# Four transformer layers in one kernel: `by` loads issued by GpSimd, another order at the ends of the feed-forwards, key norms tile by tile

## The chip, the cores and the metric

The kernel runs on one core of a Trainium2 chip. A time is the device time of one launch in microseconds, the median of three runs. Beside the timed runs there is one profiled execution, from which every row, gap and duration below is taken; the page gives its own time and its span.

The core has a matrix engine (TensorE, PE in the profile, whose weight loads are listed as PEld), a vector engine (VectorE, DVE), a scalar engine (ScalarE, ACT), a general one (GpSimd, POOL) and a queue engine (SyncE, SP) that here only issues transfers. A DMA can be issued by SyncE or by GpSimd; the profile lists the first kind's queue as hardware_dynamic and the second's as software_dynamic.

## The reference

The input x has 1024 tokens of 256 numbers. Eight stages follow one another, each `x = layernorm(x + stage(x))`: four times an attention and then a feed-forward, each pair of another design. Everything is float32.

- attn0: 16 heads, 4 key heads, window of 64, rotary positions, two softmaxes subtracted. ffn0: 8 experts, 2 per token.
- attn1: 16 heads of 128, causal, biases. ffn1: weights rounded to three values, hidden width 1024, a root mean square norm over the hidden row.
- attn2: 16 heads of 16, causal. ffn2: hidden width 2048, weights stored as 4-bit codes with a scale per 32 of them (dequantized as table value times scale), gelu gate.
- attn3: 16 query heads, 4 key heads of 128; queries and keys are divided by their root mean square over the head's 128 numbers before the scores. ffn3: 64 experts of width 64, 8 per token, and one shared expert with its own gate:

```
comb[token, expert] = top-8 probability, renormalized      # 0 for the other experts
out = sum over experts of (silu(x Wg) * (x Wu)) Wd * comb[:, expert]  +  gate * shared expert
```

ffn3 computes every expert for every token and multiplies by `comb`, which is zero where the expert was not chosen. These multipliers are called `factors` in the kernel.

## The kernel before, in words

x lies in SBUF as 8 tiles of 128 tokens, and its transpose xT, which the projections read, as 256 rows by 1024 tokens. Much is done by halves of 512 tokens (tiles 0 to 3, tiles 4 to 7). `transpose_two(t)` (L178) transposes two tiles of x on TensorE and copies them into xT (L185). `project` (L159) multiplies a weight by 512 columns of xT; `project_rows` (L166) gives rows of 128 tokens instead.

The order of work. In the attention stages it is written out by hand: `in_order` fixes the order of every engine's instructions as the program issues them. A `Pipe` there holds a list of units (the scores of one head for one tile of queries: matmul L274, maximum L254 on VectorE, exponent L259 on ScalarE, normalization L267 on GpSimd, transposition by L371 and a DMA, or by TensorE in L390 for some, and the product with values L408) and fills the matmul time that remains with other pieces of work, projections above all, by their estimated costs. In the feed-forward stages a scheduler decides the order within the program's own dependencies and priorities.

**Feed-forwards 2 and 3** share `Kit.ffn` (L289 to L323). The hidden width is cut into chunks of 128 (16 in ffn2, 33 in ffn3, the last one the shared expert). `add_up(i, half)` projects one chunk's gate and up for 512 tokens (4 matmuls of L159, which the trace shows as 8 entries), calls `hidden` for the activation, and multiplies by the down weights into two accumulators in PSUM (2 matmuls of L307, 4 entries). The loop does chunk i of the first half and chunk i - lag of the second half (lag 3 in ffn2, 4 in ffn3), so that the second half trails. At the last chunk the first half is complete: `add_ffn(acc, 0)` copies the accumulators out of PSUM (L332), transposes them on TensorE (L336), adds them to x (L240) and norms x's first half (L209, L210, L227, L228, L213). ffn1 has its own loop of the same form (L1395 to L1402) with 8 chunks and `finish(half)`, which first sums the squares of the hidden rows by matmuls and takes a root on ScalarE.

**hidden of ffn3** (L2196 to L2206): ScalarE computes silu of the gate (L2203), VectorE multiplies by up (L2204) and then by `by` (L2205). `by` is a tile of 128 rows by 512 tokens, in which the factors of the chunk's two experts stand 64 times each. It is loaded from `factors` in DRAM by a DMA whose source repeats a row 64 times (L2201): 66 loads of 256 KB, into 8 rotating buffers, issued by SyncE, which also issues the weight loads (L97). The factors are written to DRAM at the end of attn3 by the steps of the router.

**attn1** carries a second task, `beside`: the generator `ffn2_weights` dequantizes ffn2's weights long before they are used. It has 157 steps, over 24 half tiles of 128 x 512: VectorE operations L1836, L1840, L1844 and L1849, a GpSimd multiply by scales L1854, and DMAs issued by GpSimd for codes and scales (L1805, L1808, L1818, L1821) and for the result (L1859). After each of the 128 units of attn1 the loop takes one step, and two after every fourth unit.

**attn3** starts by transposing x. Its list of pieces then has, for the first half: key rows of four tiles (`make_rows`: L166, copied by L2002, squared and summed by ScalarE in L2005), values of four tiles (L166, L2033), `norm_rows` of the half, queries (L159), keys (transposed normed rows); and the same for the second half, which runs between the first units of the softmax. `norm_rows` raises the mean squares to the power -1/2 (`power`: L220 on VectorE, L221 on GpSimd, 128 x 16 for a half) and multiplies the rows by them on GpSimd (L2013, 128 x 2048 for a half). GpSimd also does two of the softmax's steps in this stage, a small product (L256) and the normalization (L267).

The stages' list in `four_layers` (L2232) says which pairs of tiles are transposed ahead of each stage: all four in attn3, none in ffn2 and ffn3.

Of the kernel before, what the change touches and what calls it, by code (L numbers as in the profile page):

```python
# [31 lines left out]
P = 128  # L32
# [10 lines left out]
class Kit:  # L43
# [245 lines left out]
    def ffn(self, chunks, count, hidden, before=iter(()), lag=LAG):  # L289

        nc = self.nc
        acc = [self.wide() for _ in range(NC)]
        held = {}

        def add_up(i, half):
            size, gate, up, down, more = held[i] if half == 0 else held.pop(i)
            g, u = self.bank()[:size], self.bank()[:size]  # L300
            self.project(g, gate, half * HALF, HALF)
            next(before, None)
            self.project(u, up, half * HALF, HALF)
            next(before, None)
            h = hidden(g, u, half, more)
            for m in range(NC):
                nc.tensor.matmul(  # L307
                    acc[m][:, half * HALF : (half + 1) * HALF],
                    lhsT=down[:, m * P : (m + 1) * P], rhs=h, start=i == 0, stop=i == count - 1,
                )  # L310

        for i in range(count + lag):
            if i < count:
                held[i] = next(chunks)
                add_up(i, 0)
            if i == lag - 1:
                for _ in before:
                    pass
            if i == count - 1:
                self.add_ffn(acc, 0)  # L320
            if i >= lag:
                add_up(i - lag, 1)
        self.add_ffn(acc, 1)  # L323

    def add_ffn(self, acc, half, scale=None):
# [740 lines left out]
def attn1(k, a):  # L1066
# [171 lines left out]
    with k.in_order(transfers=True):  # L1238
        for t in range(NT):
            two = k.tile("ot", [P, 2, D])  # L1240
            for i in range(2):
                gathered.append(two[:, i, :])
                k.gather(gathered[-1], results, slots[:, i * NT + t : i * NT + t + 1])

        for t, count in ((0, 0), (2, 3), (4, 4), (6, 5)):
            add_results(t)
            for i in range(count - 1):
                project_next()
            take_root(t)
            if count:  # L1250
                project_next()
            close(t)
        for count, (g, h, half, s) in enumerate(units):
            now[:] = g, h
            if count == 96:
                pipe.base = 1.2
            if (h, half) == (1, 0) and g < 3:
                if s == 0:
                    loading = load(g + 1)
                next(loading, None)  # L1260
            if s == 0:
                ensure(make_queries, g, 15)
                ensure(make_keys, g, h, half)
            blocks = 4 * half + s + 1
            if s % 2 == 0:
                pipe.reach(count // 2 - 3)
                pair = Pair(k, (blocks, blocks + 1), on_pe=(g, h) == (3, 3))
            pipe.unit(
                queries[g][:, h, (blocks - 1) * P : blocks * P],
                lambda lo, n: keys[g, h][:, lo : lo + n], blocks, pair, s % 2,  # L1270
                masked=g == 3,
            )
            if s % 2:
                pipe.then(attend(g, h, half, s // 2, pair))
            pipe.fill()
            for _ in range(2 if count % 4 == 3 else 1):
                next(beside, None)
        for _ in pipe.drain():
            pass
        for _ in beside:  # L1280
            k.catch_up()
        k.catch_up()
# [55 lines left out]
def ffn1(k, a):  # L1338
# [56 lines left out]
    for i in range(8 + k.LAG):  # L1395
        if i < 8:
            add_up(i, 0)
        if i == 7:
            finish(0)
        if i >= k.LAG:  # L1400
            add_up(i - k.LAG, 1)
    finish(1)  # L1402


# [494 lines left out]
def attn3(k, a):  # L1899
# [107 lines left out]
                accum_out=total[half][:, t % 4 * 4 + h : t % 4 * 4 + h + 1],  # L2007
            )

    def norm_rows(half):  # L2010
        norm = k.power(total[half], 16, 1e-6, 1.0 / 128)
        heads = raw[half].rearrange("p t (h d) -> p (t h) d", h=4)
        nc.gpsimd.tensor_tensor(  # L2013
            heads, heads, norm.unsqueeze(2).to_broadcast([P, 16, P]), ALU.mult
        )

    def make_keys(half, h):
# [48 lines left out]
        factors[g, half] = k.power(ps[:, ::32], 16, 128e-6, tag="factor")  # L2066


    pieces = [(make_rows, t) for t in range(4)]
    pieces += [(make_values, t) for t in range(4)]  # L2070
    pieces += [(norm_rows, 0)]
    pieces += [(make_queries, 0, 0, h) for h in range(4)]
    pieces += [(make_sums, 0, 0)]
    pieces += [(make_keys, 0, h) for h in range(4)]
    pieces += [(make_factors, 0, 0)]
    pieces += [(make_rows, t) for t in range(4, 8)] + [(norm_rows, 1)]
    pieces += [(make_values, t) for t in range(4, 8)]
    pieces += [(make_queries, 0, 1, h) for h in range(4)]
    pieces += [(make_sums, 0, 1)]
    pieces += [(make_keys, 1, h) for h in range(4)]  # L2080
# [89 lines left out]
def ffn3(k, a):  # L2170


    nc = k.nc

    def chunks():
        gu = wd = None
        for p in range(32):
            if p % 2 == 0:
                gu = k.weights(
                    [P, NC, 512],  # L2180
                    a["L3_ffn_gate_up"][:, p * 256 : (p + 2) * 256].rearrange(
                        "(c p) f -> p c f", p=P
                    ),
                )
            if p % 4 == 0:
                wd = k.weights([P, 4, D], a["L3_ffn_down"][:, p * D : (p + 4) * D])
            at = (p % 2) * 256
            yield (
                P, lambda c, w=gu, s=slice(at, at + P): w[:, c, s],
                lambda c, w=gu, s=slice(at + P, at + 2 * P): w[:, c, s], wd[:, p % 4, :], p,  # L2190
            )
        gu = k.weights([P, NC, P], a["L3_ffn_shared_gate_up"].rearrange("(c p) f -> p c f", p=P))
        wd = k.weights([64, D], a["L3_ffn_shared_down"])
        yield (64, lambda c: gu[:, c, :64], lambda c: gu[:, c, 64:], wd, 32)

    def hidden(g, u, half, p):  # L2196
        n = g.shape[0]

        by = k.tile("by", [P, HALF])[:n]
        rows = k.factors[2 * p : 2 * p + n // 64, half * HALF : (half + 1) * HALF]  # L2200
        nc.sync.dma_start(out=by, in_=rows.unsqueeze(1).to_broadcast([n // 64, 64, HALF]))  # L2201
        s, h = (k.tile("t2", [P, HALF])[:n] for _ in range(2))
        nc.scalar.activation(s, g, AF.Silu)  # L2203
        nc.vector.tensor_tensor(h, s, u, ALU.mult)  # L2204
        nc.vector.tensor_tensor(h, by, h, ALU.mult)  # L2205
        return h  # L2206

    k.ffn(chunks(), 33, hidden, (step for steps in k.closing for step in steps), lag=4)


# [14 lines left out]
def four_layers(ctx: ExitStack, tc: tile.TileContext, a, out):  # L2225
# [3 lines left out]
    for stage in STAGES:  # L2229
        with k.scope(**SCOPES[stage]):  # L2230

            mine = {ffn0: (), attn1: (), ffn1: (), ffn2: (), attn2: (0, 2), ffn3: ()}  # L2232
            for t in mine.get(stage, range(0, NT, 2)):
                k.transpose_two(t)
            stage(k, a)
            if stage == attn1:
                k.layernorm()
# [75 lines left out]
```

## Time and profile before

| | us |
|---|---|
| median of three runs | 2238.06 (2237.61 to 2240.51) |
| the profiled execution's own time | 2230.16 |
| its span | 2228.5 |
| TensorE busy in it | 2037.2 |
| granted TensorE clock, mean | 0.972 |

By stage, from the trace (bounds by the stages' first and last matmuls, rounded):

| stage | from, to | length | PE busy | DVE busy | ACT busy | POOL busy | DMA share |
|---|---|---|---|---|---|---|---|
| attn0 | 0, 296 | 296 | 241.8 | 230.5 | 153.0 | 106.8 | 0.38 |
| ffn0 | 296, 395 | 99 | 79.3 | 56.8 | 37.7 | 29.5 | 0.39 |
| attn1 | 395, 906 | 511 | 488.3 | 346.3 | 213.3 | 175.3 | 0.44 |
| ffn1 | 906, 967 | 61 | 54.9 | 32.8 | 36.3 | 20.1 | 0.16 |
| attn2 | 967, 1196 | 229 | 199.8 | 136.8 | 101.3 | 32.8 | 0.15 |
| ffn2 | 1196, 1379 | 183 | 176.9 | 87.3 | 45.7 | 0.0 | 0.06 |
| attn3 | 1379, 1838 | 459 | 426.6 | 295.5 | 211.8 | 157.1 | 0.35 |
| ffn3 | 1838, 2228.5 | 390.5 | 369.6 | 113.4 | 50.4 | 0.7 | 0.20 |

How to read it: busy times are microseconds within the stage; the DMA share is the mean busy share of the core's 16 DMA engines. In timeline rows the first number is the start from the span's beginning, the second the time that the row's instructions took together, then engine, line, operation, the tile written and the tiles read, the shape and how many instructions; in brackets stands how long the engine had been idle before, and what released it. SPq and POOLq rows are issues of DMAs. A row of waits gives the total, how many times, and the longest. In the 40 slices a digit is the busy share in tenths. The times of the table add to the span; the 1.7 us between the span and the execution's own time lie outside of what the trace shows.

### The profile page before, as it was taken

How to read it: one execution, taken by the hardware profiler on the slowest of the kernel's cores; microseconds unless marked ns; L12 is line 12 of the kernel's file. 1: busy time of each engine (PE TensorE's matmuls, PEld its weight loads, DVE VectorE, ACT ScalarE, POOL GpSimd, SP SyncE). 2: the span in 40 equal slices, each digit the busy share in tenths (PEclk: the TensorE clock that was granted, in tenths of full speed). 3: DMA queues.
4: the chain of work that ended last, by engine and by line, in shares of the span. 5: the costliest groups of instructions: out<-in, count | busy, mean ns of one | idle time of the engine just before them, and what ended most of it. 6: DMA issues, size and time to landing. Idle time of an engine off the chain costs nothing.

```text
span 2228.5 us, 24592 instructions
## 1 busy us (share of the span) xinstructions
PE 2037.2 (91%) x7893; PEld 1191.4 (53%) x7893; DVE 1299.4 (58%) x2588; ACT 849.6 (38%) x2230; POOL 522.3 (23%) x771
## 2 busy tenths in 40 slices
PE   7988768899999997988988998899999989999997
PEld 3655544576766665754434443466666665433343
DVE  6898756677777664456754444277777664222223
ACT  3656424453444433444462223654444441111111
POOL 5343131333333332402110000433333320000000
PEclk9999879999999999999999999999999999999998
DMA  6222443253545542105000000034355321222211
GB/s 183 76 72 58 136 130 109 64 148 102 145 108 161 144 103 78 38 29 181 1 2 10 29 30 0 24 95 111 93 141 125 91 53 63 76 76 84 76 65 44
DMA packets 152520, 186.88 MB, mean 84 GB/s; under 512 B 31460, under 2 KB 115240, under 8 KB 152392
## 3 DMA queue, kind: packets, MB, share of 16 engines
q1 hardware_dynamic: 142808, 160.25, 26.2%
q0 software_dynamic: 9584, 25.05, 3.7%
q8 instruction: 64, 1.05, 0.2%
q14 instruction: 64, 0.52, 0.1%
HBM read 85.24 MB, written 17.44 MB: 46 GB/s over the span
## 4 chain that ended last, share of the span: by engine, by line
PE 62%; DVE 9%; DMA 7%; ACT 3%; issue 3%; POOL 2%; SPq 1%; DVEq 0%; POOLq 0%; ACTq 0%
PE bank L159 19%; PE wide L274 9%; PE bank L408 8%; PE wide L307 6%; DMA by<-factors 5%; PE bank L166 4%; PE bank L1179 2%; DVE turned L371 2%; PE bank L1616 2%; PE bank L856 2%; PE bank L1019 1%; DMA pt<-turned 1%; PE bank L1354 1%; POOL p L267 1%; PE wide L1629 1%
## 5 line engine op out<-in xcount | busy, mean ns | idle before, releaser
L159 PE MATMUL bank<-xT,w 128*128 128x512 f32 (+2 forms) x1488 | 629.2, 563 | 4.1 <-DVE xT L185 3.0
L159 PEld LDWEIGHTS bank<-xT,w 128*128 128x128 f32 (+1 forms) x1488 | 283.1, 194 | 275.1 <-issue 254.3
L371 DVE STREAM_TRANSPOSE turned<-p 128x128 f32<-128x128 f32 (+7 forms) x232 | 283.5, 1222 | 76.0 <-DMA pt<-turned 40.3
L274 PE MATMUL wide<-k,q 128*128 128x512 f32 (+3 forms) x768 | 293.7, 492 | 18.3 <-ACT p L259 17.5
L267 POOL TENSOR_SCALAR p<-p,st 128x128 f32<-128x128 f32 (+7 forms) x256 | 190.5, 744 | 475.3 <-DVE st L266 474.8
L408 PE MATMUL bank<-pt,v 128*128 128x256 f32 x1216 | 279.4, 371 | 8.0 <-DMA pt<-turned 5.7
L408 PEld LDWEIGHTS bank<-pt,v 128*128 128x128 f32 x1216 | 225.9, 191 | 60.6 <-issue 21.0
L254 DVE TENSOR_REDUCE st<-wide 128x1 f32<-128x128 f32 (+7 forms) x256 | 193.4, 756 | 47.1 <-PE wide L279 40.1
L307 PE MATMUL wide<-t,w 128*128 128x512 f32 (+1 forms) x392 | 196.7, 626 | 17.0 <-DVE t L2205 11.8
L274 PEld LDWEIGHTS wide<-k,q 128*128 128x128 f32 x768 | 139.5, 191 | 135.3 <-issue 92.9
L259 ACT ACTIVATE p<-wide,st,factor 128x128 f32<-128x128 f32 (+7 forms) x128 | 106.4, 831 | 213.5 <-POOL st L256 210.6
L2204 DVE TENSOR_TENSOR t<-t,bank 128x512 f32<-128x512 f32 (+1 forms) x66 | 45.3, 686 | 238.8 <-PE bank L159 238.8
L259 ACT ACTIVATE p<-wide,st 128x128 f32<-128x128 f32 (+7 forms) x128 | 94.9, 741 | 230.1 <-DVE st L254 211.9
L2203 ACT ACTIVATE t<-bank 128x512 f32<-128x512 f32 (+1 forms) x66 | 39.4, 597 | 305.5 <-PE bank L159 279.5
L307 PEld LDWEIGHTS wide<-t,w 128*128 128x128 f32 (+1 forms) x392 | 67.8, 191 | 134.3 <-DVE t L2205 58.4
L779 ACT ACTIVATE e<-wide,st 128x128 f32<-128x128 f32 x256 | 90.0, 377 | 74.3 <-DVE st L787 65.6
L166 PE MATMUL bank<-w,xT 128*128 128x512 f32 (+2 forms) x288 | 118.0, 547 | 0.0
L249 DVE TENSOR_TENSOR wide<-wide,causal 128x128 f32<-128x128 f32 x192 | 55.9, 291 | 98.7 <-PE wide L274 97.5
L1641 ACT ACTIVATE pt<-wide 128x1024 f32<-128x1024 f32 (+3 forms) x96 | 75.6, 811 | 69.9 <-PE wide L1635 68.1
L166 PEld LDWEIGHTS bank<-w,xT 128*128 128x128 f32 x288 | 52.6, 196 | 44.0 <-issue 40.3
L1593 DVE TENSOR_REDUCE st<-wide 128x2 f32<-128x1024 f32 x64 | 64.3, 1020 | 20.0 <-PE wide L1589 10.2
L845 PE MATMUL bank<-w,ot 128*128 128x256 f32 x256 | 67.4, 411 | 6.8 <-ACT ot L839 5.5
(307 smaller groups left out, 2788.4 us busy)
## 6 DMA issues: line engine op xcount, KB each, us to landing
by<-factors SPq DMA_DIRECT2D x64, 256.0 KB
pt<-turned SPq DMA_DIRECT2D x60, 240.0 KB
pt<-turned SPq DMA_DIRECT2D x60, 176.0 KB
pt<-turned SPq DMA_DIRECT2D x156, 64.0 KB
w<-in_L_ffn_gate_up_dram SPq DMA_DIRECT2D x16, 512.0 KB
pt<-turned SPq DMA_DIRECT2D x28, 256.0 KB
pt<-turned SPq DMA_DIRECT2D x60, 112.0 KB
pt<-turned SPq DMA_DIRECT2D x28, 224.0 KB
```

The lines of the kernel that those rows point to most:

```text
L159: self.nc.tensor.matmul(out, lhsT=weight(c), rhs=self.xcols(c, lo, n), start=c == 0, stop=c == NC - 1)
L166: self.nc.tensor.matmul(out, lhsT=self.xcols(c, lo, n), rhs=weight(c), start=c == 0, stop=c == NC - 1)
L254: nc.vector.tensor_reduce(top, scores[:, :n], axis=AX.X, op=ALU.max, negate=True)
L259: nc.scalar.activation(probs[:, :n], scores[:, :n], AF.Exp, bias=top, scale=1.0 if scale is None else scale, accum_out=total,)
L267: self.nc.gpsimd.tensor_scalar(probs[:, :n], probs[:, :n], total, 1.0, ALU.mult, ALU.mult)
L274: self.nc.tensor.matmul(s[:, lo : lo + m], lhsT=query, rhs=key(lo, m), start=True, stop=not masked or lo + m < n, skip_group_check=masked,)
L307: nc.tensor.matmul(acc[m][:, half * HALF : (half + 1) * HALF], lhsT=down[:, m * P : (m + 1) * P], rhs=h, start=i == 0, stop=i == count - 1,)
L371: k.nc.vector.transpose(squares.rearrange("p b (k q) -> p b k q", q=32), probs[:, :n].rearrange("p (k i b) -> p b k i", b=4, i=32),)
L408: self.k.nc.tensor.matmul(out.rearrange("p (a q) -> p a q", q=32) if first else out.rearrange("p (s a q) -> p s a q", s=2, q=32), lhsT=val ...
L779: nc.scalar.activation(e[:, r, f, b, :], sc[:, r, f, b, :], AF.Exp, bias=top[:, at : at + 1], accum_out=total[:, at : at + 1],)
L845: nc.tensor.matmul(y, lhsT=oT[:, i % 2 * 2 + i // 2].rearrange("p b n -> p (b n)"), rhs=wo[:, i, :], start=i == 0, stop=i == 3,)
L1641: nc.scalar.activation(two[:, :, lo:], sc[:, :, lo:], AF.Exp)
```

## The change

Four edits, independent of each other.

1. In `Kit.ffn`, and likewise in ffn1's loop, the second half's piece `add_up(i - lag, 1)` comes ahead of `add_ffn(acc, 0)` (or `finish(0)`) in the last first-half round, instead of after it.
2. In attn1 the loop takes two steps of `beside` after three of every five units and one after the other two (1.6 a unit), instead of two after one of every four (1.25 a unit).
3. In attn3 `norm_rows` works on one tile (128 x 4 and 128 x 512) and comes after the next tile's rows; the second half's values come tile by tile between rows and norm. x's tiles 4 to 7 are transposed after the first half's last norm piece, instead of ahead of the stage.
4. In ffn3 the `by` loads are issued by GpSimd instead of SyncE.

```diff
@@ Kit.ffn
             if i == lag - 1:
                 for _ in before:
                     pass
+            if i >= lag:
+                add_up(i - lag, 1)
             if i == count - 1:
                 self.add_ffn(acc, 0)
-            if i >= lag:
-                add_up(i - lag, 1)
         self.add_ffn(acc, 1)
@@ attn1
             pipe.fill()
-            for _ in range(2 if count % 4 == 3 else 1):
+            for _ in range(2 if count % 5 < 3 else 1):
                 next(beside, None)
@@ ffn1
         if i < 8:
             add_up(i, 0)
+        if i >= k.LAG:
+            add_up(i - k.LAG, 1)
         if i == 7:
             finish(0)
-        if i >= k.LAG:
-            add_up(i - k.LAG, 1)
     finish(1)
@@ attn3
-    def norm_rows(half):
-        norm = k.power(total[half], 16, 1e-6, 1.0 / 128)
-        heads = raw[half].rearrange("p t (h d) -> p (t h) d", h=4)
+    def norm_rows(t):
+        half, at = t // 4, t % 4
+        norm = k.power(total[half][:, at * 4 : at * 4 + 4], 4, 1e-6, 1.0 / 128)
+        heads = raw[half][:, at, :].rearrange("p (h d) -> p h d", h=4)
         nc.gpsimd.tensor_tensor(
-            heads, heads, norm.unsqueeze(2).to_broadcast([P, 16, P]), ALU.mult
+            heads, heads, norm.unsqueeze(2).to_broadcast([P, 4, P]), ALU.mult
         )
...
-    pieces = [(make_rows, t) for t in range(4)]
+    pieces = [(make_rows, 0)]
+    for t in range(1, 4):
+        pieces += [(make_rows, t), (norm_rows, t - 1)]
     pieces += [(make_values, t) for t in range(4)]
-    pieces += [(norm_rows, 0)]
+    pieces += [(norm_rows, 3), (k.transpose_two, 4), (k.transpose_two, 6)]
     pieces += [(make_queries, 0, 0, h) for h in range(4)]
...
-    pieces += [(make_rows, t) for t in range(4, 8)] + [(norm_rows, 1)]
-    pieces += [(make_values, t) for t in range(4, 8)]
+    for t in range(4, 8):
+        pieces += [(make_rows, t), (make_values, t), (norm_rows, t)]
@@ ffn3
-        nc.sync.dma_start(out=by, in_=rows.unsqueeze(1).to_broadcast([n // 64, 64, HALF]))
+        nc.gpsimd.dma_start(out=by, in_=rows.unsqueeze(1).to_broadcast([n // 64, 64, HALF]))
@@ four_layers
-            mine = {ffn0: (), attn1: (), ffn1: (), ffn2: (), attn2: (0, 2), ffn3: ()}
+            mine = {ffn0: (), attn1: (), ffn1: (), ffn2: (), attn2: (0, 2), attn3: (0, 2), ffn3: ()}
```

## The prediction

> **What bounds the kernel now.** I read the page first, its busy table and its 40 slices:
>
> ```profile
> PE 2037.2 (91%) x7893; PEld 1191.4 (53%) x7893; DVE 1299.4 (58%) x2588; ACT 849.6 (38%) x2230; POOL 522.3 (23%) x771
> ...
> PE   7988768899999997988988998899999989999997
> ...
> PE 62%; DVE 9%; DMA 7%; ACT 3%; issue 3%; POOL 2%; SPq 1%; DVEq 0%; POOLq 0%; ACTq 0%
> ```
>
> TensorE is the bound almost everywhere: 2228.5 - 2037.2 = 191 us is all that it stands still, and no edit removes a matmul. So the question is which of its gaps each edit closes or opens. By the DMA's 7% of the chain I went to the last stage (1838 to 2228), with busy time by stretch (length, PE, PEld, DVE, ACT, POOL, clock, DMA share, GB/s), SyncE's timeline and the waits:
>
> ```profile
> 1890.00:1895.00 5.00, 5.00 (x12) 2.01 (x11) 1.38 (x2) 0.60 (x1) 0.00 (x0) 1.00 0.13 51
> 1957.00:2143.00 186.00, 176.91 (x397) 72.51 (x396) 45.51 (x66) 19.70 (x33) 0.00 (x0) 1.00 0.23 79
> ```
>
> ```profile
> 1957.90 4.93 SPq L97 DMA_DIRECT2D w<-in_L_ffn_down_dram  x1
> 1962.91 14.87 SPq L2201 DMA_DIRECT2D by<-factors  x4
> 1977.88 7.09 SPq L97 DMA_DIRECT2D w<-in_L_ffn_gate_up_dram  x1
> ```
>
> ```profile
> DVE t L2205 <- DMA by<-factors: 12.6, 20, 1.8
> PE wide L307 <- DVE t L2205: 11.8, 14, 1.6
> ```
>
> One half chunk takes PE about 5.27 us. In the first stretch only `by` transfers run: a DMA share of 0.13 is 2 of 16 engines, and 256 KB at 51 GB/s is 5.0 us each. Sixty-six of them take 330 us; the weight loads interleave on the same engines, so SyncE blocks, `by` comes late, and PE idles 9.1 us between 1957 and 2143.
>
> Next the fourth attention's start and its second half of rows, by the timeline:
>
> ```profile
> 1382.84 1.79 PE L178 MATMUL bank<-ident,x 128*128 128x128 f32 x8 [2.66 <-DVE x L213]
> ...
> 1425.76 2.90 POOL L221 TENSOR_TENSOR st<-st,minus_half 128x16 f32<-128x16 f32 x1 [1.37 <-DVE st L220]
> ...
> 1428.75 3.61 POOL L2013 TENSOR_TENSOR raw<-raw,st 128x2048 f32<-128x2048 f32 x1
> ...
> 1433.71 1.22 PE L274 MATMUL wide<-k,q 128*128 128x256 f32 x2 [6.50 <-ACT p L259]
> ...
> 1434.72 5.50 PE L166 MATMUL bank<-w,xT 128*128 128x512 f32 x8
> ```
>
> GpSimd is blocked 6.5 us by the norm of four tiles; the softmax waits for its small operations, and PE waits for the softmax. Last, the ends of the third feed-forward and the tail of the second attention:
>
> ```profile
> 1346.30 3.68 PE L307 MATMUL wide<-t,w 128*128 128x512 f32 x4 [2.39 <-DVE t L1893]
> ...
> 1373.38 3.51 PE L307 MATMUL wide<-t,w 128*128 128x512 f32 x4 [2.39 <-DVE t L1893]
> ```
>
> ```profile
> 853.51 1.28 POOL L1854 TENSOR_TENSOR decoded<-sign,scales 128x512 f32<-128x512 f32 x1
> ...
> 857.25 0.61 POOL L1859 DMA_DIRECT2D decoded_down<-decoded  x1 [2.46 <-issue]
> ...
> 858.33 0.47 PE L390 MATMUL bank<-ident,p 128*128 128x128 f32 x1 [6.06 <-POOL p L267]
> ```
>
> **What the Trainium skill says.** "DMA: Bandwidth & Descriptors", section "Why a DMA increments its semaphore by 16 and not by 1": the number of engines k is the largest up to 16 that divides both slowest dimensions; a hardware-generated DMA takes the lowest-numbered k, one from GpSimd's queue k consecutive ones from a rotating cursor. `by` is 2 x 64 rows, so k = 2, and the share of 0.13 agrees; the cursor no row of before shows. Against it, the same page's "Issuing engines are not separate DMA queues": issuing elsewhere saves only issue time. "SBUF — State Buffer", "SBUF: two separate sides": VectorE operations in a two-port mode can lock GpSimd out while it writes descriptors. The trace shows 256 KB issues on GpSimd at 0.58 to 0.70 us in the second attention, where VectorE is about 70% busy, but also the 2.46 us above. "TensorE: Matmul & The Clock Gate", Part 1, The HAM clock gate: an idle window of some 3.4 us halves TensorE's clock for as long. It agrees: eight L166 matmuls took 5.50 us after the 6.5 us gap, 3.43 to 3.60 elsewhere.
>
> **Part 4, `by` on GpSimd's queue.** SyncE loses 66 issues and keeps the weight loads; GpSimd gains 66 issues, 66 x 0.65 = 43 us of 390, in a stage where it is idle but for two small powers (L221). In the built order five `by` issues stand ahead of the second power, each of those free at once: 5 x 0.65 = 3.3 us from 1838, against that power's start at about 1850, so it isn't delayed. Later issues wait for VectorE's use of the buffer eight earlier (8 x 5.27 = 42 us of lead) and for the eighth earlier transfer; only more `by` issues are behind them. If successive transfers rotate over engine pairs, none is late, and the gain is the 9.1 us less some that matmul starts would lose anyway. From the waits: 11.8 us of L307 on L2205, of which 2 x 1.56 us belong to the stage's two ends, leaves **-8.7**. Without the cover (the same two engines) it is 66 x 5.0 plus 25 weight shares of 1.25 = 361 us against 348 of PE: late as now, 0. Both ends kept: 0 to -9.5, and below a loss, in the rivals.
>
> **Part 3, fourth attention.** Start: eight transposes of x (tiles 4 and 6) now wait 2.66 us for the third feed-forward's last norm, with the first projections queued behind. L178 for tiles 0 and 2 ended at 1380.2; the projections began at 1384.42. Afterwards they wait only for the copy of xT at about 1381.6, and the transposes cost 1.1 us later. 1384.42 - 1381.6 - 1.1 = **-1.7**. Norm: per tile a power of 128x4, between 0.70 us (the trace's 128x2) and 2.90 (128x16), say 1.0, and a multiply of 128x512, 1.27 as L1854: 2.3 us a tile, four of them, on GpSimd between the softmax's small steps. 9.2 us is more than 6.5, but in pieces, with rows and values between. Units there take about 2.6 us, set by ScalarE (2.2 of rows, 0.45 of exponent), so a 2.3 us block mostly fits. Walked by hand, the ninth unit's exponent starts about 20 us after the first's instead of 26, less the one value piece (1.72 us) that no longer fills: **-4.6**, including the slow clock. Bad end: each block delays 2.6 us more, total 0; good end -8. The first half's norm lies under value projections on both sides. PE is nearly 100% busy from 1460 to 1600, so what is gained stays. Together **-6.3**.
>
> **Part 1, order at ends.** Third feed-forward: two gaps of 2.39 us (L307 behind L1893), and the matmuls after them took 3.68 and 3.51 us instead of 1.9. With the second half's piece ahead of add_ffn, its projections (2.6 us) lie under the first gap; the tail's projections likewise. What is late next: the copy and transposes (L332, L336), by one piece, which norm x's first half later; that lies under the remaining second-half pieces. Of 2 x (2.39 + 1.7) = 8.2 us perhaps four tenths: **-3.5** (-1 to -6). Second feed-forward: its gaps there are 0.4 to 1.7 us; the root on ScalarE now stands behind other evictions: **0** (-1.5 to +2). Fourth: a gap of 1.56 us moves from one L307 to another, **-0.4**; the first half's output leaves 5 us later, not at the end.
>
> **Part 2, denser dequantization in the second attention.** 157 steps at 1.6 a unit instead of 1.25 end at unit 98, not 126 of 128. The last 100 us lose VectorE's L1836 to L1849 and GpSimd's L1854 and L1859; the transpose of 858.33 starts near 855.4: **-3** (-1 to -5). The same work comes 28% denser in 419 to 775, where VectorE rises from 72% to about 75% and PE stood only 5.7 us: +0.5 (0 to +2; +7 if the queue of small steps on GpSimd shows there as it did at 858). **-2.5**.
>
> **Sum.** -8.7 - 6.3 - 3.5 + 0 - 0.4 - 2.5 = -21.4, rounded to -22 with part 4's upper end. Against the profiled execution's own 2230.16 us (span 2228.5 and 1.7 around it): 2208. That execution is 7.9 us under the median of 2238.06; I take the difference as the same there: **2216**.
>
> **Rivals.** A, the change doesn't do what it says: GpSimd's transfers land on the same two engines; for it the skill's sentence on shared queues, against it the cursor. Part 4 gives 0: 2238 - 13 = 2225. B, slower: GpSimd's `by` transfers are served one after another, each with a fixed delay; from 370/66 = 5.6 us each they fall behind PE's 348 us and the rest. Lone GpSimd loads of 256 KB took 3.7 to 9.2 us to land. At 7 us each the stage needs 462 us, +90: about 2310 with the other gains. Against it: several can be under way at once. C, attention gives back: the four small norms hold GpSimd as long as one large one, or the denser dequantization costs the second attention 5 us net; the norm blocks speak for it. -22 + 6: 2222 to 2224. D, A and C together: 2231 to 2235.
>
> **How the numbers follow.** Forecast 0.42, A 0.18, C 0.18, D 0.10, B 0.12. Measurement can tell about 0.2%, 4.5 us. Forecast, A, C and a third of D are faster: 0.81; the rest of D is same: 0.07; B is slower: 0.12. The range, 2205 to 2233, takes the forecast's own (2206 to 2221), A, C and part of D.
>
> **What would show it.** Part 4: no wait of L2205 for `by`, PE full from 1957 to 2143 (rival A: the same 12 us of waits; B: `by` among the largest waits, landing over 5.6 us apart). Part 3: no 6.5 us gap by 1433, L166 at 3.5 us, norm pieces of about 2.3 us. Part 1: L307 groups at 1.9 us at the third feed-forward's end. Part 2: L1854 gone after about 780, the 6.06 us gap under 4. I am wrong above all if GpSimd's descriptors or its engine choice are slower than its issues in the second attention suggest.

## The result

The changed kernel takes 2211.65 us (median of four runs, 2209.61 to 2214.76), the kernel before 2237.84 us beside it: a ratio of 0.9883, 95% interval 0.987 to 0.9896. That is 26 us, or 1.2%, less. The changed kernel's profiled execution took 2209.61 us, its span is 2207.9 us. The two profiled executions differ by 20.5 us only, because that of the kernel before (2230.16 us) lay 7.9 us under the median of 2238.06 of its three runs before the prediction, and that of the changed kernel 2.0 us under 2211.65.

The page of the changed kernel, busy times, slices and the chain by engine:

```profile
PE 2032.4 (92%) x7893; PEld 1195.5 (54%) x7893; DVE 1300.5 (59%) x2594; ACT 848.9 (38%) x2230; POOL 578.2 (26%) x849
...
PE   7988768899999899988898999999999989999997
...
PE 68%; DVE 9%; DMA 3%; ACT 3%; POOL 2%; issue 2%; SPq 1%; DVEq 0%; ACTq 0%; POOLq 0%
```

TensorE's work is the same 7893 instructions and 5 us less of busy time; its idle time fell from 191.3 to 175.5 us. DMA's share of the chain fell from 7% to 3%. So most of the time, 15.8 us, came out of gaps, as forecast; the rest is shorter matmul time. But the total hides a loss. Measured from the first instruction of one stage to that of the next, in the two profiled executions:

| stretch | before | after | difference |
|---|---|---|---|
| start to the second attention's first projection | 395.4 | 395.0 | -0.4 |
| second attention | 511.4 | 522.9 | **+11.5** |
| second feed-forward (ffn1) | 64.0 | 64.5 | +0.5 |
| third attention (no edit touches it) | 224.0 | 221.0 | -3.0 |
| third feed-forward (ffn2) | 181.0 | 175.7 | -5.4 |
| from its last L307 to the fourth attention's first projection | 8.6 | 5.3 | -3.2 |
| fourth attention, to the first silu of the last stage | 466.2 | 457.4 | -8.8 |
| last feed-forward, from there to the end | 377.8 | 366.3 | -11.6 |
| sum | 2228.5 | 2207.9 | -20.5 |

The stages of parts 3 and 4 and the third feed-forward gave more than was forecast. The second attention, with the denser dequantization, took 11.5 us longer where 2.5 us of gain had been put down. The 3.0 us of the third attention, which has no edit, show how much a stage can differ between two executions.

**Last stage.** Busy time by stretch of the changed kernel (length, PE, PEld, DVE, ACT, POOL, clock, DMA share, GB/s), its waits (total, times, longest) and the landing of the `by` loads (from L2204, now GpSimd's):

```profile
1841.60:2160.00 318.40, 318.01 (x736) 133.08 (x735) 88.26 (x146) 39.34 (x65) 48.00 (x62) 1.00 0.28 78
```

```profile
POOL by L2204 <- DVE t L2208: 236.8, 53, 5.0
...
PE wide L307 <- DVE t L2208: 3.3, 3, 1.6
```

```profile
DMA to landing us min/median/max: 3.0/7.6/13.1
```

TensorE stands 0.4 us in 318. VectorE's wait for `by` is gone from the large waits; now GpSimd waits for VectorE, that is for a free buffer, which is the healthy way round. One load lands 7.6 us after its issue although one is consumed every 5.3 us: the loads overlap.

**Fourth attention.** GpSimd's and TensorE's timelines of the changed kernel:

```profile
1423.09 1.02 POOL L221 TENSOR_TENSOR st<-st,minus_half 128x4 f32<-128x4 f32 x1 [0.17 <-DVE st L220]
1424.19 1.04 POOL L2014 TENSOR_TENSOR raw<-raw,st 128x512 f32<-128x512 f32 x1
1425.20 0.48 POOL L267 TENSOR_SCALAR p<-p,st 128x256 f32<-128x256 f32 x1
```

```profile
1384.26 14.00 PE L166 MATMUL bank<-w,xT 128*128 128x512 f32 x32 [1.47 <-DVE xT L185]
1426.58 0.70 PE L274 MATMUL wide<-k,q 128*128 128x256 f32 x2 [1.45 <-ACT p L259]
```

A tile's norm blocks GpSimd for 2.1 us, and the largest wait of TensorE for the softmax there is 1.45 us, where it had been 6.50. The granted clock is 1.00 from 1384 to 1458; in the kernel before it was 0.84 and 0.82 in the two stretches of 10 us from 1425 on.

**Third feed-forward.** TensorE's timeline at its two ends:

```profile
1359.09 1.98 PE L307 MATMUL wide<-t,w 128*128 128x512 f32 x4 [0.78 <-DVE t L1893]
...
1377.52 1.98 PE L307 MATMUL wide<-t,w 128*128 128x512 f32 x4 [0.78 <-DVE t L1893]
```

Each gap is 0.78 us instead of 2.39, and the matmuls after it take 1.98 us instead of 3.68 and 3.51.

**Second attention.** Here is the loss. GpSimd's timeline at one place, TensorE's gaps after it and at a second place, and TensorE's wait for the transposed probabilities over the softmax part of the stage (421 to 890):

```profile
719.78 0.59 POOL L1859 DMA_DIRECT2D decoded_gate<-decoded  x1 [0.30 <-POOL decoded L1854]
720.37 0.63 POOL L1818 DMA_DIRECT2D scales<-in_L_ffn_up_scales_dram  x1
720.99 0.57 POOL L103 DMA_DIRECT2D w<-ternary_up  x1
```

```profile
729.53 3.48 PE L408 MATMUL bank<-pt,v 128*128 128x256 f32 x16 [3.64 <-DMA pt<-turned]
761.27 5.17 PE L408 MATMUL bank<-pt,v 128*128 128x256 f32 x16 [3.88 <-DMA pt<-turned]
```

```profile
PE bank L408 <- DMA pt<-turned: 11.2, 5, 3.9
```

Three transfers of 256, 256 and 512 KB leave GpSimd within 1.3 us, while SyncE has just issued four transposing transfers of probabilities and is about to issue four small ones. Those that the trace times landed after 5.5 to 7.5 us, against medians of 5.0 us (240 KB) and 3.6 us (48 KB) over the stage. The same wait in the kernel before is 2.2 us. Between the first and the last exponent of the stage TensorE's idle time grew from 14.3 to 20.2 us, and the busy time of the same 1677 matmuls from 441.8 to 445.9 us.

### The profile page after: what moved, and what is told of

It reads as the page before. It is cut to its first block, busy times and chain, and to the rows that moved or that the text cites. A ratio compares the mean times of both kernels' runs of the same rounds, so it can differ in the third digit from the quotient of the medians.

```text
span 2207.9 us, 24613 instructions
## 1 busy us (share of the span) xinstructions
PE 2032.4 (92%) x7893; PEld 1195.5 (54%) x7893; DVE 1300.5 (59%) x2594; ACT 848.9 (38%) x2230; POOL 578.2 (26%) x849
## 2 busy tenths in 40 slices
DMA packets 177928, 187.11 MB, mean 85 GB/s; under 512 B 61028, under 2 KB 144808, under 8 KB 177800
## 4 chain that ended last, share of the span: by engine, by line
PE 68%; DVE 9%; DMA 3%; ACT 3%; POOL 2%; issue 2%; SPq 1%; DVEq 0%; ACTq 0%; POOLq 0%
PE bank L159 22%; PE wide L274 9%; PE bank L408 9%; PE wide L307 8%; PE bank L166 4%; PE bank L1179 3%; DMA pt<-turned 2%; DVE turned L371 2%; PE bank L1616 2%; PE bank L856 2%; PE bank L1019 1%; PE bank L1354 1%; POOL p L267 1%; PE wide L1629 1%; ACT pt L1641 1%
## 5 line engine op out<-in xcount | busy, mean ns | idle before, releaser
L371 DVE STREAM_TRANSPOSE turned<-p 128x128 f32<-128x128 f32 (+7 forms) x232 | 283.6, 1222 | 89.4 <-DMA pt<-turned 47.9
L267 POOL TENSOR_SCALAR p<-p,st 128x128 f32<-128x128 f32 (+7 forms) x256 | 190.5, 744 | 477.6 <-DVE st L266 476.8
L274 PE MATMUL wide<-k,q 128*128 128x512 f32 (+3 forms) x768 | 293.5, 492 | 12.6 <-ACT p L259 11.6
L307 PE MATMUL wide<-t,w 128*128 128x512 f32 (+1 forms) x392 | 193.7, 617 | 4.9 <-DVE t L2208 3.3
L259 ACT ACTIVATE p<-wide,st 128x128 f32<-128x128 f32 (+7 forms) x128 | 94.8, 741 | 241.1 <-DVE st L254 213.0
L259 ACT ACTIVATE p<-wide,st,factor 128x128 f32<-128x128 f32 (+7 forms) x128 | 106.3, 831 | 206.2 <-POOL st L256 206.0
L307 PEld LDWEIGHTS wide<-t,w 128*128 128x128 f32 (+1 forms) x392 | 67.1, 189 | 118.4 <-issue 49.8
L2204 POOL DMA_DIRECT2D by<-factors x66 | 51.7, 789 | 260.1 <-DVE t L2208 236.8
## 6 DMA issues: line engine op xcount, KB each, us to landing
pt<-turned SPq DMA_DIRECT2D x28, 224.0 KB, 3.9
```

What stands on the lines that cost most here:

```text
L259: nc.scalar.activation(probs[:, :n], scores[:, :n], AF.Exp, bias=top, scale=1.0 if scale is None else scale, accum_out=total,)
L267: self.nc.gpsimd.tensor_scalar(probs[:, :n], probs[:, :n], total, 1.0, ALU.mult, ALU.mult)
L274: self.nc.tensor.matmul(s[:, lo : lo + m], lhsT=query, rhs=key(lo, m), start=True, stop=not masked or lo + m < n, skip_group_check=masked,)
L307: nc.tensor.matmul(acc[m][:, half * HALF : (half + 1) * HALF], lhsT=down[:, m * P : (m + 1) * P], rhs=h, start=i == 0, stop=i == count - 1,)
L371: k.nc.vector.transpose(squares.rearrange("p b (k q) -> p b k q", q=32), probs[:, :n].rearrange("p (k i b) -> p b k i", b=4, i=32),)
```

## The experiments

All are edits of the changed kernel. They ran on several chips, on which the kernel before took 2237.8 to 2244.0 us, so totals are compared as ratios to it. Beside the ratio stand stretches of the profiled execution, which tell the parts apart much better than the totals do. "Softmax of attn1" is from the first to the last exponent (L259) of the second attention.

| kernel | ratio, 95% interval | softmax of attn1 | ffn2 | to attn3 | attn3 | ffn3 |
|---|---|---|---|---|---|---|
| before | 1 | 456.1 | 181.0 | 8.6 | 466.2 | 377.8 |
| changed | 0.9883 (0.987, 0.9896) | 466.1 | 175.7 | 5.3 | 457.4 | 366.3 |
| part 2 undone | 0.9845 (0.9819, 0.9871) | 459.4 | 174.7 | 5.3 | 456.7 | 366.5 |
| part 4 undone | 0.9935 (0.9915, 0.9956) | 465.7 | 174.7 | 5.3 | 454.6 | 377.0 |
| part 3 undone | 0.9948 (0.9937, 0.996) | 466.1 | 175.6 | 8.2 | 466.4 | 364.8 |
| part 1 undone | 0.99 (0.9875, 0.9926) | 469.3 | 181.1 | 5.8 | 455.2 | 364.4 |
| norm by halves, x late | 0.9918 (0.9902, 0.9935) | 464.5 | 174.8 | 5.3 | 464.9 | 365.2 |
| `by` by SyncE, 64 rows | 0.9892 (0.987, 0.9914) | 464.7 | 174.6 | 5.3 | 456.5 | 365.6 |
| no code loads, dense | 0.9847 (0.9829, 0.9865) | 456.8 | 175.9 | 5.3 | 455.2 | 365.3 |
| dense, other phase | 0.9913 (0.9893, 0.9933) | 464.7 | 174.6 | 5.3 | 455.0 | 366.3 |
| no code loads, sparse | 0.9853 (0.9834, 0.9871) | 457.0 | 174.9 | 5.3 | 454.3 | 366.6 |
| steps by half, 1.25 | 0.988 (0.9861, 0.9899) | 457.3 | 174.7 | 5.3 | 454.5 | 364.9 |
| steps by half, 1.5 | 0.9848 (0.9828, 0.9869) | 456.4 | 174.7 | 5.3 | 456.5 | 365.6 |

Each of the last four columns moves only where the edit of its stage is undone, wholly or in part, and is otherwise within about 3 us in all the variants: the four parts hardly act on each other. The four parts undone alone change the median by 12.9 + 15.2 + 4.9 - 7.6 = 25.4 us, of 26.2 for all together.

**Each part undone alone.** Part 2:

```diff
-            for _ in range(2 if count % 5 < 3 else 1):
+            for _ in range(2 if count % 4 == 3 else 1):
```

> The changed kernel with part 2 alone undone (1.25 steps of the dequantization a unit in the second attention, as before). Theory from the two traces: part 2 cost time, because the denser steps put GpSimd's stores, scale loads and weight reloads on top of the probabilities' transposing transfers: the second attention went from 511.4 to 522.9 us between its first projection and the third stage's first matmul. Then this kernel has that stretch at 511 to 512 us and takes about 11 us less than the changed kernel: about 2200. Rival, the prediction's: part 2 gains 2.5 us, so undoing it gives 2214; the 11 us would then be an accident of one execution.

2204.08 us on a chip where the kernel before took 2238.84, 7.6 us less than the changed kernel's 2211.65. The softmax of the second attention took 459.4 us instead of 466.1, and TensorE's wait for the probabilities fell from 11.2 to 2.8 us (the same view, the same stretch):

```profile
PE bank L408 <- DMA pt<-turned: 2.8, 2, 1.9
```

The theory holds, with 7.6 us instead of 11: the whole stage took 514.7 us, not 511 to 512, and the total 2204, not 2200. The rival's +2.5 us is out. By medians this kernel is faster than the kernel before and the changed one; its ratio's interval just touches that of the changed kernel.

Part 4:

```diff
-        nc.gpsimd.dma_start(out=by, in_=rows.unsqueeze(1).to_broadcast([n // 64, 64, HALF]))
+        nc.sync.dma_start(out=by, in_=rows.unsqueeze(1).to_broadcast([n // 64, 64, HALF]))
```

> The changed kernel with part 4 alone undone (by loads issued by SyncE again). Theory: two fixed engines carry all by transfers, so the 12 us of waits of VectorE for by are back; the last stage from its first silu to the end takes 377 to 378 us again instead of 366.3, the kernel 2222 to 2224. Rival: the gain of that stage came from part 1's order at its end, and this kernel stays within 3 us of the changed one (2212 to 2215).

2224.59 us, ffn3 377.0 us. The waits of its last stage:

```profile
DVE t L2208 <- DMA by<-factors: 12.3, 19, 1.8
...
PE wide L307 <- DVE t L2208: 12.0, 14, 1.6
```

They are those of the kernel before, so the gain of the last stage is part 4's. From first silu to 47.9 us ahead of its end, a tail that is equally long in both kernels, this kernel needs 329.1 us where the changed one needs 318.4 (its row stands above):

```profile
1845.90:2175.00 329.10, 319.85 (x734) 133.12 (x733) 88.25 (x146) 39.34 (x65) 0.40 (x1) 1.00 0.21 74
```

Of the 10.7 us, 8.9 are idle time of TensorE (9.25 against 0.39). The other 1.8 are busy time, with two matmuls fewer and the clock at 1.00: the first L307 behind a wait adds 0.70 us of busy time, any other 0.46, on average.

Part 3 was undone as a whole: `norm_rows` on a half, its two places in the list as before, all four transposes of x ahead of the stage.

```diff
-    pieces += [(norm_rows, 3), (k.transpose_two, 4), (k.transpose_two, 6)]
+    pieces += [(norm_rows, 0)]
...
-    for t in range(4, 8):
-        pieces += [(make_rows, t), (make_values, t), (norm_rows, t)]
+    pieces += [(make_rows, t) for t in range(4, 8)] + [(norm_rows, 1)]
+    pieces += [(make_values, t) for t in range(4, 8)]
```

> The changed kernel with the whole of part 3 undone (norm of four tiles at once, all transposes of x ahead of the stage). Theory: the 6.5 us gap with its slow clock behind the norm of the second half is back, and 1.7 to 2.7 us of wait for the third feed-forward's last norm: the fourth attention from its first row projection to the last stage's first silu takes 464 to 467 us instead of 457.4, and its start comes 2 to 3 us later; in all 2219 to 2222. Rival: the small norms only spread the same GpSimd time, and most of the 8.8 us came from clock windows that fell elsewhere: 2213 to 2216.

2226.82 us, beyond the expected 2219 to 2222: 15.2 us more than the changed kernel. The two stretches agree with the expectation, 466.4 and 8.2 us; they make 11.9 us of the difference between the two profiled executions. TensorE's timeline shows the old gap and the slow matmuls behind it again:

```profile
1437.85 1.22 PE L274 MATMUL wide<-k,q 128*128 128x256 f32 x2 [6.50 <-ACT p L259]
1438.86 5.46 PE L166 MATMUL bank<-w,xT 128*128 128x512 f32 x8
```

The rival, a shift of clock stretches only, is out: the gap comes and goes with the edit.

Part 1, both loops:

```diff
-            if i >= lag:
-                add_up(i - lag, 1)
             if i == count - 1:
                 self.add_ffn(acc, 0)
+            if i >= lag:
+                add_up(i - lag, 1)
```

> The changed kernel with part 1 alone undone in both loops (add_ffn or finish of the first half ahead of the second half's piece). Theory: the third feed-forward has its two 2.4 us gaps and two half-clock windows back, 5.4 us; the second feed-forward is the same within 1 us, the last within 1 us: about 2217. Rival, the prediction's size: 3.9 us, about 2215.5.

2216.54 us, 4.9 more than the changed kernel. The intervals of the two ratios overlap, so the total doesn't settle it; the stretches do. ffn2 took 181.1 us, its two gaps and the matmuls after them as before:

```profile
1360.82 3.62 PE L307 MATMUL wide<-t,w 128*128 128x512 f32 x4 [2.40 <-DVE t L1893]
...
1387.85 3.63 PE L307 MATMUL wide<-t,w 128*128 128x512 f32 x4 [2.39 <-DVE t L1893]
```

ffn1 is the other way: 64.0 and 64.6 us in the two kernels with the old order, 64.5 to 66.7 (median 65.95) in the eleven with the new one. The new order costs about 1.6 us there.

**Part 3 taken apart.** The norm by halves as before, but the transposes of x late:

```diff
-    pieces += [(norm_rows, 3), (k.transpose_two, 4), (k.transpose_two, 6)]
+    pieces += [(norm_rows, 0), (k.transpose_two, 4), (k.transpose_two, 6)]
```

> The changed kernel with the norm of keys again by halves (128x16 and 128x2048) and the second half's values again behind it, but x's tiles 4 to 7 still transposed after the first half's norm. Against the kernel with all of part 3 undone (2226.8) it tells the two edits of part 3 apart. Theory from the traces: the moved transposes are worth the 2.9 us by which the fourth attention's first projection came earlier, the small norms about 9 of the 9 us after it; so 2223 to 2225 here. Rival: the transposes shifted the whole front of the stage and are worth half or more of part 3: 2217 to 2219.

The ratio of 0.9918 lies between 0.9948 and 0.9883, with intervals of about 0.0015 to each side: 6.7 us for the transposes, 7.8 us for the norm. By stretches the transposes gave 2.9 us ahead of the stage and 1.4 in it (466.4 to 464.9), the norm 7.5 to 10 us (464.9 to 457.4 or, as the median of the ten kernels with small norms, 455.2). So the norm is the larger part by the stretches, though these are of single executions; the totals don't exclude the rival's half for the transposes.

**Why `by` was late.** SyncE again, but with a source that divides otherwise:

```diff
-        rows = k.factors[2 * p : 2 * p + n // 64, half * HALF : (half + 1) * HALF]
-        nc.gpsimd.dma_start(out=by, in_=rows.unsqueeze(1).to_broadcast([n // 64, 64, HALF]))
+        for i in range(n // 64):
+            row = k.factors[2 * p + i : 2 * p + i + 1, half * HALF : (half + 1) * HALF]
+            nc.sync.dma_start(out=by[64 * i : 64 * i + 64], in_=row.to_broadcast([64, HALF]))
```

> The changed kernel with by loaded by SyncE again, but as two DMAs of 64 rows, each with one expert's row repeated, instead of one DMA of two rows repeated 64 times (132 issues instead of 66, the same bytes). Theory: what was late before is the two engines that a 2-row source gets; 64 rows divide by 16, so each load spreads over 16 engines, lands early, and VectorE never waits for by: the kernel takes 2209 to 2214, as with GpSimd's queue, and a stretch with by loads alone shows the same bytes but SyncE's issues at about 0.5 us instead of 4.7. Rival: what counted was that by and the weights shared SyncE's queue; then the waits stay and it takes 2222 to 2226.

0.9892, the same as the changed kernel, and ffn3 365.6 us. The line's own answer from the trace (duration of the issue in ns, then landing) has:

```profile
L2205 SPq DMA_DIRECT2D by<-factors x130: 444/588/603, 1838.3 to 2156.5; - x130
...
DMA to landing us min/median/max: 2.7/2.9/3.2
```

In a stretch with `by` transfers alone, as the one from 1890 to 1895 in the prediction was (DMA share 0.13, 51 GB/s), this kernel has:

```profile
1880.00:1890.00 10.00, 10.00 (x24) 4.17 (x23) 2.76 (x4) 1.19 (x2) 0.00 (x0) 1.00 0.40 141
```

An issue takes 0.59 us instead of 4.7, and a load lands in 2.9 us. A DMA share of 0.40 is more than two of 16 engines can give. VectorE doesn't wait for `by` at all. SyncE issues twice as many transfers beside the weights on the same queue, and nothing is late: the queue was not the cause, the two engines of a two-row source were. This agrees with what the Trainium skill's "DMA: Bandwidth & Descriptors", section "Why a DMA increments its semaphore by 16 and not by 1", says of the number of engines: 16 divides 64 rows and not two. GpSimd's queue was one cure, another shape is as good.

**Why the dense dequantization cost time.** With 11 of 12 loads of codes and scales left out:

```diff
             if i == 1 and after:
-                packed = load_codes(*after)
+                pass
...
             if i == 1 and after:
                 yield
-                scales = load_scales(*after)
+                pass
```

> The changed kernel, dense dequantization as it is, but codes and scales are loaded once, for the first of the twelve weight blocks, and used for all twelve: it leaves out 11 loads of codes and 11 of scales, and computes the third feed-forward with wrong weights. All VectorE and GpSimd arithmetic and the stores stay. Theory: part 2 costs time because these transfers collide with the probabilities' transposing transfers; without them the second attention takes 511 to 515 us instead of 522.9, the kernel 2201 to 2205. Rival: the cost is the arithmetic and the multiplies on GpSimd between the softmax's steps; then it stays at 521 to 523 us and 2209 to 2213.

The softmax part took 456.8 us, as in the kernel before, at the full density of the arithmetic, and the ratio is 0.9847, that of the kernel with part 2 undone. TensorE's wait:

```profile
PE bank L408 <- DMA pt<-turned: 4.2, 2, 2.6
```

(The whole stage took 518.0 us, above the expected 511 to 515: on the chips of this and the later experiments, and of the two before it, the first exponent came 31.4 to 32.2 us after the first projection instead of 26.3, whatever the kernel. The expectations of whole stages don't allow for these 5 us, which is why the table counts from the exponent on. Why they came stays open.) So the rival, arithmetic between the softmax's steps, is out. The edit leaves out the loads of codes and of scales together, and takes their issues of about 0.6 us each from GpSimd as well. That these issues, between the softmax's steps, were the cost is not supported by the waits: VectorE's for GpSimd's normalization (L371 on L267) is 17.9 us in the changed kernel, still 15.0 without the loads, and 15.9 in the last kernel below, which loses nothing either; TensorE's own wait for GpSimd (L390 on L267) is 4.1 us in the changed kernel and 9.1 in the kernel before. The same with sparse steps:

> As the kernel that leaves out 11 of 12 loads of codes and of scales (and so computes the third feed-forward with wrong weights), but with the dequantization at 1.25 steps a unit, as before the change. It tells whether the loads cost time at any density, or only when they are dense. Theory: at 1.25 the transfers mostly fit between the probabilities' transfers, so leaving the loads out gains at most 3 us on the changed kernel with sparse steps: second attention 511 to 515 us, ratio to the kernel before 0.983 to 0.985. Rival: every load costs the transposing transfers about the same; then the stretch falls by 7 us as it did at the dense setting, to 506 to 509, ratio 0.981 or less.

457.0 us and 0.9853: leaving the loads out gains nothing worth measuring on the 456.1 and 459.4 us of the two kernels with sparse steps and loads. The loads cost time only where they are dense.

Another phase of the same density:

```diff
-            for _ in range(2 if count % 5 < 3 else 1):
+            for _ in range(2 if count % 5 > 1 else 1):
```

> The changed kernel with the same 1.6 steps a unit, but two steps after units 2, 3 and 4 of every five instead of after 0, 1 and 2. Theory: the loss is set by which stores and loads meet which of the transposing transfers, so another phase moves it by some us either way: second attention between 514 and 526 us, total 2203 to 2215, with the gaps of TensorE before the products with values at other units than 729 and 761 us. Rival: the density alone sets it: 522 to 524 us and the same total as the changed kernel within 2 us.

464.7 us, as the other dense kernels (464.5 to 469.3): which step of five is double doesn't matter, and nothing shows of the spread that the theory allowed. Its ratio, 0.9913, is above the changed kernel's 0.9883 by more than the stretches explain; why stays open.

Then the place of the steps, by halves. Units of the first half have 1 to 4 blocks of keys, those of the second 5 to 8, with the larger transfers:

```diff
-            for _ in range(2 if count % 5 < 3 else 1):
+            for _ in range(2 if half == 0 else s % 2):
```

> The changed kernel with ten dequantization steps in every eight units (1.25 a unit, as before the change), but two after each unit of the first half, whose transposing transfers are small (1 to 4 blocks), and one after every other unit of the second half (5 to 8 blocks). Theory, collisions of transfers: fewer stores and loads meet large transfers, and the second attention is no longer than with even steps, 508 to 515 us; the kernel at a ratio of 0.981 to 0.985. Rival: the steps are 2 a unit in half of the units, dense there, and what counts is VectorE and GpSimd between the short units' softmax steps: 517 to 525 us, ratio 0.987 to 0.990.

```diff
-            for _ in range(2 if count % 5 < 3 else 1):
+            for _ in range(2 if half == 0 else 1):
```

> The changed kernel with two dequantization steps after units of the first half and one after units of the second (1.5 a unit; done by unit 105). Theory, collisions with large transfers: the second halves carry no more than before the change, so the loss is at most half of the dense setting's: second attention 513 to 519 us, ratio 0.983 to 0.987. Rival, the overall density sets it: 519 to 524 us, ratio 0.987 to 0.989.

457.3 and 456.4 us. The second of them does 1.5 steps a unit and loses nothing. Its wait of TensorE for the probabilities is the smallest of those shown:

```profile
PE bank L408 <- DMA pt<-turned: 0.7, 3, 0.3
```

So neither density alone nor phase sets the loss: 1.5 steps a unit cost nothing where the denser ones stand in the units whose own transfers are small. The opposite placement, dense steps in the units with large transfers alone, was not run. With 0.9848 this kernel, too, is faster than the changed one.

The first kernel's total, 0.988, is higher than its stretches say, outside what was expected and inside what its rival named. Its profiled execution, 2207.14 us, is the fastest of its four by 5 us, so its stretches speak for that execution alone. Its third attention took 226.2 us, as in the two other kernels on that chip (226.5 us), so that isn't the reason, which stays open. The conclusion rests on the second kernel, whose total and stretches agree.

## Why the prediction was right or wrong

The time, 2216 us forecast and 2211.65 measured, and the direction were right. That the sum came so near is in part luck. By medians parts 3 and 4 gave 13 us more than forecast, and part 2 came out 10 us worse. The -22 stood for the profiled execution, where the difference is 20.5 us; the 7.9 us by which the kernel before lay under its median were carried over to the changed kernel, which lay only 2.0 us under its own.

- **Part 4, -8.7 us.** The mechanism was right in each step: two engines, VectorE late by a total of 12 us, cured by spreading. It was worth 12.9 us by medians, 10.7 by the stretch. The term was short by the 1.8 us of longer matmuls behind waits, which a sum of waits leaves out. The GpSimd issue took 0.78 us in the median, not 0.65, at no cost; none took over 0.93 us, so no lock-out by VectorE shows. Rivals A and B did not happen: that issuing elsewhere saves only issue time, on which A rested, doesn't fit the 10.7 us gained here. That GpSimd's transfers take turns over engine pairs was not shown as such: no view used here tells engines apart. Shown is that they overlap and that spreading is enough.
- **Part 3, -6.3 us.** Right in kind, half of the size: 15.2 us by medians, 12 to 14 by stretches (2.9 ahead of the stage and 9 to 11 in it). The step that failed is the walk from the first to the ninth exponent, 26 us to 20 less one value piece, which by itself makes 4.3 and leaves 0.3 of the 4.6 for the slow clock. The trace of before has 27.3 us for the 26; the changed kernel needs 18.6, no piece was missing, and by the seventeenth unit the lead is 11.5 us. From the first projection to the end of the disturbed part (1384 to 1470 before, 1384 to 1458 after) TensorE has 7.2 us less of idle time and 4.7 us less of busy time, the second because some 10 us at half clock are gone (granted clocks of 0.95, 0.84 and 0.82 in three stretches before, 1.00 after). The slow clock was priced far too low. The block of 2.3 us was 2.1.
- **Part 1, -3.9 us.** 4.9 us by medians, with overlapping intervals. By stretches ffn2 gave 5.4 to 6.4 us rather than 3.5: both gaps shrank by 1.6 us and both slow stretches went, which makes 2 x 1.6 + 2 x 1.7 = 6.6; the "four tenths" was a guess in place of that sum. ffn1 cost 1.6, inside its bounds of -1.5 to +2. In the last stage the 1.56 us gap moved to another L307, as said.
- **Part 2, -2.5 us.** Wrong in sign: it cost 7.6 us by medians, 6.7 in the softmax part against the kernel with part 2 undone and 10.0 against the kernel before. The gain at the tail was there: from unit 112 to unit 127 the changed kernel is 3.4 us faster, forecast -3. What failed is the step "The same work comes 28% denser ... +0.5": from the first unit to unit 112 the changed kernel lost 13.5 us. The step counted VectorE's share (72% to 75%) and TensorE's idle time, and took GpSimd's small steps for the worst case. The runs show the transfers instead: TensorE's wait for them grew by 9.0 us, and the loss went with the loads. Their mean share doesn't tell, 0.41 to 0.60 by stretches of 50 us before; at one place (713 to 719) the engines were nearly full even then. Rival C named a cost of 5 us for the denser work, without the transfers as its cause.
- The chain of rivals was complete for direction, but none of them stood for what came: two parts larger, one about as forecast and one reversed.

## What to carry to other kernels

When background work is made denser, ask which of its transfers share the DMA engines with transfers that the bound engine waits for, and put them beside the units whose own transfers are small; engine shares don't show this. Look for loads that repeat a few rows: here one of two rows kept two of 16 engines busy, and issues of 4.7 us on its queue were the sign; splitting it into loads of 64 rows was as good as moving it to another queue. A wait of TensorE cost its length here, plus 0.24 us for the first matmul behind it, plus, where it came, half of a slow-clock stretch of 3.4 us: price all three.

## What the runs showed that was not expected

- The clock fell to half for 3.4 us behind gaps shorter than that: behind 2.39 us twice in ffn2 before (3.68 and 3.51 us for matmuls of 1.98), but not behind the 0.78 us of after. The Trainium skill's "TensorE: Matmul & The Clock Gate", Part 1, speaks of an idle window of about 3.4 us; here a gap of seven tenths of that was enough. But the length of a gap doesn't decide it alone: the 3.64 us at 729.53 in the changed kernel had no slow clock behind it (3.48 us for the 16 matmuls), the 3.88 us at 761.27 had (5.17 us). So what a gap costs by the clock can differ from one kernel or execution to the next.
- The third attention, which no edit touches, took 221.0 to 229.3 us in the profiled executions of the changed variants, and 224.0 before. In the changed kernel's profile it was 3.0 us shorter than before, with about 6 us less at half clock in the trace's record of the clock. Differences of a few us in one stage of one execution can't be put down to an edit unless they recur.
- The page of the changed kernel counts 177,928 packets, 25,408 more than before, and 29,568 more of under 512 bytes, for the same data: GpSimd's 66 loads bring many small packets with them. They cost this stage nothing that shows: it took 366.3 us, and 365.6 with the loads of 64 rows on SyncE.
- A power on GpSimd of 128x4 took 1.02 us, between 0.70 (128x2) and 2.90 (128x16), and a multiply of 128x512 by a repeated column 1.04.
